# Ordinary identity matmuls in TensorE's planned gaps, ahead of the first scan and behind the last

## The chip, the cores and the metric

The kernel runs on one core of a Trainium2 chip. The core has a matrix engine (TensorE: PE, with its weight loads shown apart as PEld), VectorE (DVE), ScalarE (ACT), GpSimd (POOL) and SyncE (SP), which issues DMAs; POOL issues some DMAs too. The metric is the device time of one launch in microseconds, the median of several runs. A profile is one further execution with the hardware profiler on; its span goes from the first to the last instruction.

## The reference

The input is 8 batches of 1024 tokens with 256 features, in float32. Three blocks follow one another, each added to its input:

```
x = x + 0.5 * ffn(layernorm(x))
x = x + mamba(layernorm(x))
x = x + 0.5 * ffn(layernorm(x))

ffn:   gate = q(x) @ q(w_gate).T ;  up = q(x) @ q(w_up).T        # 256 -> 704
       out  = q(silu(gate) * up) @ q(w_down).T                   # 704 -> 256
       # q: blocks of 16 along the last axis, each rounded to an FP4 grid times (max |x| / 6)
mamba: x, z = split(norm(h) @ in_proj)                           # 256 -> 512 + 512
       x = silu(causal_conv4(x)) ; dt, B, C = split(x @ x_proj)  # 64 + 16 + 16
       delta = softplus(dt @ dt_proj + b)
       h_t = exp(delta_t * A) * h_(t-1) + delta_t * B_t * x_t    # per channel (512) and state (16)
       y_t = sum_n C_t[n] * h_t[n] + D * x_t ;  out = (y * silu(z)) @ out_proj
```

The recurrence over 1024 tokens runs on its own for every batch, channel and state.

## The kernel before

The tokens are cut into 16 chunks of 512, two to a batch. A chunk passes through five stages, written as generators: `stage_f1` (first feed-forward block, tiles `f_*`), `stage_m1` (norm, input projection, convolution, `x_proj`, `dt_proj`; tiles `m_*`), `stage_z` (the gate branch), `scan` (tiles `s_*`) and `stage_out` (output projection, tiles `o_*`, and the second feed-forward block, whose tiles are named `f_*` again). Ahead of all that, `prep_up` and `prep_down` quantize and transpose the weights (`w_ld`, `w_t`), and `prep_mamba` loads and scales the others.

In the scan, for each of 16 states and each of 4 groups of 128 channels, ACT forms `s_bu` (L793) and the decay `s_da` (L797), TensorE transposes `s_bu` into PSUM (`s_pb`, L800, against the identity `ident`), and DVE runs the recurrence over 512 tokens in one instruction (`s_h`, L802). POOL multiplies by C (L810) and adds the result to DRAM with an accumulating DMA (`accd`, L835).

In a feed-forward block, ACT normalizes (`f_xn`), `quant` rounds it with DVE, ACT and POOL in turn (L459 to L469), TensorE transposes (`f_pt`, L547), multiplies by both weights (`f_pg`, `f_pu`, L559, in two halves of 352 columns, two matmuls each), transposes the quantized product (`f_pa`, `f_pb`, L571 and L575) and multiplies by the down weights (`f_po`, L579, six matmuls of 256 columns). In the profile an ordinary float32 matmul is two records, a transpose is one.

All instructions are recorded first, and then `set_order` fixes the order of each engine. `Graph` collects the dependencies and prices every instruction (`price`), and `plan` is a list scheduler over the engines: it walks forward with priorities, then back and forward again, `PASSES` times, and the plan with the shortest total by its own prices is kept. Each engine's instructions are then chained in that order by dependencies without a semaphore. So each engine takes its instructions strictly in the planned order and waits wherever an operand isn't there yet.

The planner knows of TensorE's clock: it counts the columns that pass in each `TICK` (3413 ns), a transpose as half an ordinary matmul, and where the tick before had fewer than `WARM` columns, it doubles the price of the TensorE instruction:

```
if not back and e == ET.PE:
    if passed[t // TICK - 1] < WARM:
        more = hold
    passed[(t + hold + more) // TICK] += cols
    free[e] += more
```

Two PSUM buffers, pool `psb`, hold the transposes `s_pb` of the scan. `ident` is made by POOL as the first thing in the program.

## Time and profile before

| | us |
|---|---|
| runs shown (3) | 2523.82, 2534.21, 2535.66 |
| median | 2534.21 |
| the profiled execution | 2536.37 |
| its span | 2534.4 |
| PE busy | 2344.9 (93%) |
| DVE busy | 2184.4 (86%) |
| ACT busy | 2146.9 (85%) |
| POOL busy | 2177.2 (86%) |
| first transpose on TensorE (w_t, L490) starts | 19.05 |
| first scan instruction (L802) starts | 158.92 |
| last scan instructions (L802, two merged) | 2445.72, for 2.45 |

The mean granted TensorE clock is 0.985 of full speed. In a timeline, rows that follow each other with the same line and tiles are merged (xN, the time from the first start to the last end), and the brackets show the idle time ahead of the row and what ended it. In views of stretches, the columns are the stretch, its length, the busy time of each engine asked for (with its instructions), the granted clock (PEclk), the share of the DMA engines and the GB/s that they moved. The chain of waits follows the work back from the last instruction to what released each step.

### The profile page before, as it was taken

To read this page: it belongs to the slowest core of one execution; us is meant where nothing else is said; L and a number is where in the kernel's file an instruction comes from. 1 tells how busy PE (TensorE), PEld (TensorE's weight loads), DVE (VectorE), ACT (ScalarE), POOL (GpSimd) and SP (SyncE) were. 2 spreads that over 40 slices of the span, in tenths; PEclk is the share of its full clock that TensorE was granted. 3 is DMA by queue.
4 is the path that set the end of the run, shared out by engine and by line. 5 is a ranking of instruction groups with operands and counts; after the bars stand their busy time and mean duration, and the time that the engine had idled before them with its cause. 6 is when DMAs were issued, how large, how long until landed. Compare 5 with 4: busy or idle time off the path is not lost.

```text
span 2534.4 us, 33625 instructions
## 1 busy us (share of the span) xinstructions
PE 2344.9 (93%) x10980; PEld 1591.6 (63%) x10980; DVE 2184.4 (86%) x3082; ACT 2146.9 (85%) x3952; POOL 2177.2 (86%) x1556
## 2 busy tenths in 40 slices
PE   5989898999999999999999999999999999888876
PEld 3555565766666666666666666666666666655544
DVE  7568797998989899898989899898989989878885
ACT  4489787998989988999888989898989988999842
POOL 4359798899989999899998999899997999899952
PEclk9989999999999999999999999999999999999998
DMA  3049779699888988789897998889896988999950
GB/s 90 9 117 207 194 163 223 163 186 238 166 197 195 218 202 189 205 171 239 176 219 173 201 221 176 211 173 221 195 202 181 189 225 175 216 235 211 232 127 17
DMA packets 113647, 465.57 MB, mean 184 GB/s; under 512 B 14592, under 2 KB 32896, under 8 KB 76864
## 3 DMA queue, kind: packets, MB, share of 16 engines
q0 software_dynamic: 36576, 266.35, 56.3%
q1 hardware_dynamic: 76896, 197.08, 24.2%
q8 instruction: 86, 1.41, 0.2%
q14 instruction: 89, 0.73, 0.1%
HBM read 146.19 MB, written 317.19 MB: 183 GB/s over the span
## 4 chain that ended last, share of the span: by engine, by line
POOL 36%; PE 27%; issue 11%; DVE 9%; ACT 9%; DMA 8%; POOLq 0%; SPq 0%; DVEq 0%; ACTq 0%
POOL s_h L810 20%; PE f_pg L559 4%; PE f_pu L559 4%; PE f_po L579 4%; PE s_pb L800 4%; POOL accd L835 4%; DVE s_h L802 4%; DMA accd<-s_h 3%; PE m_pc L682 3%; POOL f_h L462 3%; POOL f_h L469 3%; ACT s_bu L793 2%; ACT s_da L797 2%; POOL f_xn L469 2%; POOL o_y L771 2%
## 5 line engine op out<-in xcount | busy, mean ns | idle before, releaser
L810 POOL TENSOR_TENSOR s_h<-s_h,s_cbc 128x1024 f32<-128x1024 f32 x512 | 1281.8, 2596 | 51.7 <-ACT s_carry L828 27.0
L797 ACT ACTIVATE s_da<-m_delta,an 128x512 f32<-128x512 f32 x1024 | 714.5, 715 | 44.5 <-DVE s_h L802 42.8
L793 ACT ACTIVATE s_bu<-m_duT,m_bc 128x512 f32<-128x512 f32 x1024 | 693.4, 715 | 15.6 <-PE s_pb L800 14.1
L800 PEld LDWEIGHTS s_pb<-ident,s_bu 128*128 128x128 f32 x4096 | 498.0, 142 | 330.2 <-issue 123.4
L800 PE MATMUL s_pb<-ident,s_bu 128*128 128x128 f32 x4096 | 639.2, 277 | 50.9 <-DVE s_h L802 47.4
L802 DVE TENSOR_TENSOR_SCAN s_h<-s_da,s_carry,s_pb 128x512 f32<-128x512 f32 x512 | 636.5, 1265 | 16.5 <-PE s_pb L800 13.3
L802 DVE TENSOR_TENSOR_SCAN s_h<-s_da,s_pb 128x512 f32<-128x512 f32 x512 | 604.4, 1206 | 35.0 <-PE s_pb L800 21.1
L579 PE MATMUL f_po<-wdn,f_ht 128*128 128x256 f32 x1536 | 393.1, 387 | 11.5 <-ACT f_ht L576 6.8
L559 PE MATMUL f_pg<-wg,f_xt 128*128 128x352 f32 x1024 | 370.5, 473 | 13.7 <-ACT f_xt L549 6.2
L559 PE MATMUL f_pu<-wu,f_xt 128*128 128x352 f32 x1024 | 365.6, 468 | 14.1 <-DVE f_h L563 8.4
L579 PEld LDWEIGHTS f_po<-wdn,f_ht 128*128 128x128 f32 x1536 | 276.1, 192 | 73.3 <-ACT f_ht L576 17.0
L835 POOL DMA_DIRECT2D accd<-s_h x238 | 230.7, 969 | 31.8 <-POOL s_h L810 24.1
L559 PEld LDWEIGHTS f_pu<-wu,f_xt 128*128 128x128 f32 x1024 | 182.6, 193 | 115.7 <-issue 34.5
L682 PE MATMUL m_pc<-m_xp,cdg 128*128 128x512 f32 x512 | 252.7, 595 | 2.4 <-ACT m_car L679 2.4
L469 POOL TENSOR_TENSOR f_h<-f_h,q_sc 128x704 f32<-128x704 f32 x128 | 206.5, 1616 | 54.9 <-DVE f_h L468 50.5
L559 PEld LDWEIGHTS f_pg<-wg,f_xt 128*128 128x128 f32 x1024 | 180.3, 195 | 93.4 <-issue 15.1
L462 POOL TENSOR_TENSOR f_h<-f_h,q_rc 128x704 f32<-128x704 f32 x120 | 184.9, 1541 | 22.7 <-DVE q_rc L461 21.9
L563 DVE SCALAR_TENSOR_TENSOR f_h<-f_h,f_pg 128x352 f32<-128x352 f32 x256 | 128.7, 506 | 86.4 <-ACT f_h L562 85.5
L460 POOL TENSOR_SCALAR q_sc<-q_mx 128x44 f32<-128x44 f32 (+2 forms) x198 | 98.0, 497 | 88.5 <-DVE q_mx L459 83.8
L564 DVE TENSOR_TENSOR f_h<-f_h,f_pu 128x352 f32<-128x352 f32 x256 | 129.5, 507 | 41.6 <-PE f_pu L559 39.9
L562 ACT ACTIVATE f_h<-f_pg 128x352 f32<-128x352 f32 x256 | 115.6, 456 | 48.1 <-PE f_pg L559 46.6
L776 PE MATMUL o_po<-outw,o_y 128*128 128x256 f32 x512 | 129.3, 387 | 5.5 <-POOL o_y L771 2.9
(110 smaller groups left out, 3299.6 us busy)
## 6 DMA issues: line engine op xcount, KB each, us to landing
accd<-s_h POOLq DMA_DIRECT2D x238, 1024.0 KB, 9.7
s_cbc<-cd SPq DMA_DIRECT2D x128, 512.0 KB, 5.6
accd<-m_ud SPq DMA_DIRECT2D x64, 256.0 KB, 9.3
accd<-s_h SPq DMA_DIRECT2D x16, 1024.0 KB, 6.8
szd<-m_tz SPq DMA_DIRECT2D x64, 256.0 KB, 6.8
o_y<-accd SPq DMA_DIRECT2D x16, 1024.0 KB, 9.9
o_y<-accd POOLq DMA_DIRECT2D x16, 1024.0 KB, 9.1
o_sz<-szd SPq DMA_DIRECT2D x30, 512.0 KB, 5.1
```

Of the source, the lines that this page charges most:

```text
L462: mul0.tensor_tensor(vb, vb, rc.unsqueeze(2).to_broadcast([P, g, BLK]), ALU.mult)
L469: mul1.tensor_tensor(vb, vb, sc.unsqueeze(2).to_broadcast([P, g, BLK]), ALU.mult)
L559: nc.tensor.matmul(dst, xt[:, c, :], w[:, c, hf * FH : (hf + 1) * FH], start=(c == 0), stop=(c == 1))
L564: nc.vector.tensor_tensor(hh, hh, pu, ALU.mult)
L579: nc.tensor.matmul(po, ht[:, k, :], wdn[:, k, :], start=(k == 0), stop=(k == NF - 1))
L682: nc.tensor.matmul(pc, cdg[:, dc, k, :], xp[:, k : k + n], start=(k == 0), stop=(k == KC - 1))
L793: nc.scalar.activation(b, duT[s][t], AF.Copy, scale=bcol[s][:, t, k : k + 1])
L797: nc.scalar.activation(da, delta[s][dc], AF.Exp, scale=an[:, dc, k : k + 1])
L800: nc.tensor.transpose(pb[:, t * P : (t + 1) * P], bu[t][:, dc * P : (dc + 1) * P], ident)
L802: nc.vector.tensor_tensor_scan(h[:, dc, :], da, pb, init, ALU.mult, ALU.add)
L810: eng_c.tensor_tensor(hv, hv, cbc.unsqueeze(1).to_broadcast([P, cm, n]), ALU.mult)
L835: nc.gpsimd.dma_start(accd[s][j, :, :, :n], h, accum_op=ALU.add)
```

## The change

132 matmuls of `ident` by `ident` (128 columns, float32, not in transpose mode) are added on TensorE, 80 at the start of the program and 52 at its end. All 80 write one PSUM tile from `psb`, all 52 another, and nothing reads them. They are left out of the graph that the planner orders. When its order is found, `set_order` looks at the planned gaps of TensorE: for each gap of over 350 ns that lies ahead of the first planned scan instruction, or over 2000 ns behind the start of the last, it puts `FILL` (half) of the gap's time, at 213 ns each, in front of the instruction that ends the gap. The first gap is taken to begin 2.2 ticks before the first TensorE instruction. What is left of the 80 goes ahead of everything, and what is left of the 52 behind everything.

The planner's doubled price for a thin tick now holds only once the first scan is planned and until the last one is. Elsewhere a TensorE instruction is priced at full clock.

```diff
--- before.py
+++ after.py
@@ -88,6 +88,8 @@
 PORT = 200
 SLACK = 20000
 WARM = 3060
+KEEP = (80, 52)
+FILL = 0.5
 BANK = 1 << 30
 LAG = {
     (ET.DVE, ET.DVE): 127, (ET.DVE, ET.PE): 130, (ET.DVE, ET.Activation): 120, (ET.DVE, ET.Pool): 150,
@@ -179,6 +181,7 @@
         self.eng = [i.engine for i in insts]
         self.engines = sorted(set(self.eng), key=str)
         self.dma = [type(i).__name__ == "InstDMACopy" for i in insts]
+        self.scan = [bool(getattr(i, "is_tensor_tensor_scan", False)) for i in insts]
         self.cost = []
         pred = [{} for _ in insts]
         users, seen = defaultdict(list), defaultdict(list)
@@ -271,6 +274,7 @@
         dma_free = 0.0
         held, holder = 0.0, None
         passed = defaultdict(float)
+        scans = [0, sum(self.scan)]
         for x in range(self.n):
             if not left[x]:
                 heapq.heappush(wait[eng[x]], (0.0, x))
@@ -312,11 +316,13 @@
                 held, holder = t + hold, e
             start[x] = t
             order.append(x)
+            if self.scan[x]:
+                scans = [scans[0] + 1, scans[1] - 1]
             if not queued:
                 free[e] = t + hold
             more = 0.0
             if not back and e == ET.PE:
-                if passed[t // TICK - 1] < WARM:
+                if scans[0] and scans[1] and passed[t // TICK - 1] < WARM:
                     more = hold
                 passed[(t + hold + more) // TICK] += cols
                 free[e] += more
@@ -337,19 +343,40 @@
 
 def set_order(tc, tags, nbuf):
     insts = [i for i in tc.nc.cur_bb.bb.instructions if type(i).__name__ != "BassTilePoolBoundary"]
+    idle = [i for i in insts if i.engine == ET.PE and "keep" in extent([a for a in i.outs if hasattr(a, "bass_ap")][0])[0]]
+    names = {i.name for i in idle}
+    insts = [i for i in insts if i.name not in names]
     g = Graph(insts, tags, nbuf)
     path = g.paths()
     found = [g.plan([x - WEIGHT * path[x] for x in range(g.n)])]
     for _ in range(PASSES):
         total, _, start = g.plan([-s - c[0] for s, c in zip(found[-1][2], g.cost)], back=True)
         found.append(g.plan([total - s - c[0] for s, c in zip(start, g.cost)]))
-    prev = {}
-    for x in min(found, key=lambda f: f[0])[1]:
-        e = g.eng[x]
-        if e in prev:
-            tc.add_manual_dep(insts[x], insts[prev[e]].name, mybir.DependencyInfo(
+    _, order, start = min(found, key=lambda f: f[0])
+    seqs = defaultdict(list)
+    for x in order:
+        seqs[g.eng[x]].append(x)
+
+    scans = [start[x] for x in order if g.scan[x]]
+    seq, pe = [], seqs.pop(ET.PE)
+    left = list(KEEP)
+    at = start[pe[0]] - 2.2 * TICK
+    for x in pe:
+        gap = start[x] - at
+        k = 0 if start[x] < scans[0] else 1 if at > scans[-1] + 2000 else None
+        if k is not None and gap > 350:
+            n = min(left[k], int(FILL * gap / 213))
+            left[k] -= n
+            seq += [None] * n
+        seq.append(insts[x])
+        at = start[x] + g.cost[x][0]
+    spare = iter(idle)
+    chain = [i or next(spare) for i in [None] * left[0] + seq + [None] * left[1]]
+    chains = [chain] + [[insts[x] for x in u] for u in seqs.values()]
+    for u in chains:
+        for i, j in zip(u, u[1:]):
+            tc.add_manual_dep(j, i.name, mybir.DependencyInfo(
                 mybir.DependencyClass.NoSync, mybir.DependencyReason.DATA), reason="issue order")
-        prev[e] = x
 
 
 @with_exitstack
@@ -404,6 +431,13 @@
     make_identity(nc, ident)
     mhalf = const.tile([P, NT], F32, name="mhalf")
     nc.gpsimd.memset(mhalf, -0.5)
+
+    def keep_warm(n):
+        w = psb.tile([P, T], F32, tag="psb", name="keep")
+        for _ in range(n):
+            nc.tensor.matmul(w[:, :P], ident, ident, start=True, stop=True)
+
+    keep_warm(KEEP[0])
 
     def cload(shape, src, name):
         t = const.tile(shape, F32, name=name)
@@ -861,6 +895,7 @@
         spread(stage_out(s), t0 + T_O, t0 + T_O + d, pf + 3, K_O if s >= S - KE else 1)
     for _, _, gen, kind[0] in sorted(work, key=lambda w: w[:2]):
         next(gen, None)
+    keep_warm(KEEP[1])
     set_order(tc, tags, nbuf)
```

In the built program, the keeps stand on TensorE as follows, in the stretch to the second `f_pt` and at the end (xN: so many instructions; the tiles' operands are left out):

```
keep x29, w_t x4, keep, w_t x2, keep x8, w_t x4, keep, w_t x2, keep x3, w_t x4, keep, w_t x2, keep x5,
w_t x4, keep, w_t x2, keep x3, f_pt x4, keep x2, f_pg x2, f_pu x4, f_pg x2, w_t, keep, w_t, f_pg x2,
w_t x4, keep, w_t x4, keep, w_t x2, f_pu x3, f_pg x2, f_pu, keep x9, f_pt x4, keep x2, f_pg x2, ...
...
f_pu x2, f_pg x2, f_pu x2, keep x2, f_pa x4, keep x2, f_pb x2, keep, f_po x6, o_po x2, keep, f_pa x4,
keep x2, f_pb x2, o_po, f_po x6, o_po x2, f_pa x4, o_po, keep, f_pb x2, keep, f_po x6, o_po x10,
keep x20, f_pt x4, keep x2, f_pg x2, f_pu x3, f_pg x2, f_pu, f_pg x2, f_pu x2, f_pg x2, keep x9, f_pu x2,
keep x3, f_pt x4, keep x2, f_pg x2, ... f_po x6, keep, f_po x6, keep, f_pa x4, f_pb x2, keep, f_po x6, keep x3
```

## The prediction

> **What bounds the kernel now.** I read first the page's summary of the 40 slices and its chain of waits.

> ```profile
> PE 2344.9 (93%) x10980; PEld 1591.6 (63%) x10980; DVE 2184.4 (86%) x3082; ACT 2146.9 (85%) x3952; POOL 2177.2 (86%) x1556
> ...
> PE   5989898999999999999999999999999999888876
> ...
> PEclk9989999999999999999999999999999999999998
> ...
> POOL 36%; PE 27%; issue 11%; DVE 9%; ACT 9%; DMA 8%; POOLq 0%; SPq 0%; DVEq 0%; ACTq 0%
> ```

> No engine is full: four of them stand at 85 to 93%, and the chain changes engine all the time. From 160 to 2447 us (scans running) the time is therefore set by how well the orders of all engines fit each other. The granted TensorE clock is near full there. Only ahead of the first scan (158.92 us) and behind the last (2448.2 us) are other engines slack and TensorE starved, so there I looked at stretches of the clock.

> ```profile
> 47.50:51.50 4.00, 0.80 (x6) 0.91 0.00 0
> 51.50:58.00 6.50, 6.50 (x12) 0.53 0.01 3
> ...
> 74.90:77.50 2.60, 0.97 (x7) 1.00 0.00 0
> 77.50:82.00 4.50, 4.48 (x13) 0.62 0.00 0
> ```

> The columns are the stretch, its length, TensorE's busy time, the granted clock, and DMA. After 4.0 us with six transposes the clock is at 0.53; after 2.6 us with a few of them it is at 0.62. What that costs is in TensorE's timeline:

> ```profile
> 46.27 1.35 PE L559 MATMUL f_pu<-wu,f_xt 128*128 128x352 f32 x4
> 50.13 0.66 PE L547 MATMUL f_pt<-ident,f_xn 128*128 128x128 f32 x4 [2.52 <-POOL f_xn L469]
> 51.47 2.71 PE L559 MATMUL f_pg<-wg,f_xt 128*128 128x352 f32 x4 [0.69 <-ACT f_xt L549]
> 53.98 2.55 PE L559 MATMUL f_pu<-wu,f_xt 128*128 128x352 f32 x4
> 56.33 1.98 PE L559 MATMUL f_pg<-wg,f_xt 128*128 128x352 f32 x4
> ...
> 2483.20 1.12 PE L547 MATMUL f_pt<-ident,f_xn 128*128 128x128 f32 x4 [7.80 <-POOL f_xn L469]
> 2485.01 2.71 PE L559 MATMUL f_pg<-wg,f_xt 128*128 128x352 f32 x4 [0.69 <-ACT f_xt L549]
> ...
> 2498.09 2.71 PE L559 MATMUL f_pu<-wu,f_xt 128*128 128x352 f32 x4 [3.09 <-DVE f_h L564]
> ```

> The same four records take 1.35 to 1.45 us warm and 2.71 cold. The clock view reads 1.00 in the first 40 us although f_pg at 33.31 also takes 2.71, so in that stretch I go by durations.

> Dense transposes do not bring the clock back: from 166.8 to 177.0 us TensorE is 92% busy with them (9.40 of 10.20 us) at a granted 0.50. The keep matmuls are ordinary ones, so they should count.

> **The gains, part by part.** In the chain of waits, the cold pieces ahead of the first scan are:
> - a, 31.5 to 38: f_pt 1.13 against 0.67, f_pg 2.71 against 1.45, f_pu 1.79 against 1.18: 2.33 us.
> - b, 51.5 to 58: 2.71 against 1.45, 2.35 and 1.77 against 1.18 each: 3.02 us.
> - c, f_po at 77.52: 4.54 against 2.86: 1.68 us.
> - d, f_po at 146.19: 4.54 against 2.86: 1.68 us.

> Behind the last scan: f_pu and o_po at 2450 (1.7 us), f_pt and f_pg at 2483 with the start of f_pu (1.87 us), and f_pu at 2498 (1.26 us). All together 13.5 us, half a percent: the most that the clock can give here.

> **Which of them the keeps reach.** A keep waits for nothing but ident, so it runs at the front of its gap, not spread over it. From the rows, spacing goes with columns: f_pg 352 columns 0.59 us, f_po 256 columns 0.43, m_pc 512 columns 0.86. A keep of 128 columns is then 0.215 us warm and 0.43 cold. No row shows an ordinary 128-column matmul, and each comes with two weight loads (median 0.190 us each), so the other bound is 0.38 warm. I take 0.215, as f_po's records run every 0.215 us with their loads beside them, and keep 0.38 for the range. In the built order:
> - 29 keeps stand ahead of everything. ident is ready at 1.3 us, so they are done by 13.8 us even when cold, and w_t starts at 19.05. They should do nothing.
> - 25 keeps lie among and behind the 24 w_t transposes. Before, that stretch (19.05 to 31.5) has 6.8 us of work and 5.7 idle. They fit warm (5.4 us) but not cold (10.75); the clock should come up half way. Gain a 2.33 us, cost 0.3.
> - 9 keeps ahead of the second f_pt and 2 behind it fill 2.4 of 4.0 us. Gain b in full, 3.02.
> - 3 keeps after f_po and one after f_pb cut c's stretch without ordinary matmuls from 2.6 to about 1.6 us. Gain 1.68. They fit the waits of 1.18 and 0.47 us.
> - 4 keeps stand behind f_pt and f_pa, ahead of m_dt: 2.1 us are left uncovered before them, so I count half of d, 0.84, and a delay of m_dt of 0.45 (0.86 us of keeps in a wait of some 0.4).
> - Single keeps: three among the L506 transposes (waits of 0.39 and 0.20), 0.2; one ahead of m_pd where there was no wait, 0.2; the others fit their waits.
> - Tail: none stands ahead of f_pu at 2450, gain 0. Two ahead of f_pa, where TensorE had no wait, cost 0.43; two ahead of f_pb, twice, in waits of 0.31 us, cost 0.24.
> - 20 keeps after o_po end near 2479.7 and leave 3.5 us idle up to f_pt, more than the 2.6 that was enough at c. Gain 0, bounds 0 and 1.87.
> - 9 keeps ahead of f_pu at 2498 leave 1.2 of 3.09 us. Gain 1.26.
> - Three behind the last f_po end 0.65 us after 2529.7, and the span ends at 2534.4: nothing.

> Gains 2.33 + 3.02 + 1.68 + 0.84 + 1.26 = 9.13; costs 0.3 + 0.45 + 0.2 + 0.2 + 0.43 + 0.24 = 1.82. Net 7.3 us saved. With 0.38 us a keep, the costs go to about 9 us (4.0 among w_t, 0.9 ahead of the second f_pt, 1.2 at m_dt, 0.9 at f_pb, the rest in small pieces) and the gains to 11.8, as 20 keeps would then fill the 7.8 us: net 2.6.

> The front saving should pass through: from 82 to 143 us TensorE is busy 60.36 of 61.40 us, it carries the chain, and the first scan waits for its transposes.

> The keeps' two PSUM tiles come from the two-buffer psb pool. The s_pb on the same buffer stands behind all keeps in TensorE's own queue, and the tail's keeps come after the last scan's read: no wait is added. No DMA, and no instruction of another engine, is added.

> [...] At c, 2.6 us without ordinary matmuls halved the clock. [...]

> **What moves.** The planner is a list scheduler, and its prices at both ends changed: TensorE instructions after a thin window cost double before, and now only between the scans. So it gives other orders everywhere. Between the built programs, 64% of TensorE's instructions in the first tenth stand at the same position, and 38 to 59% in the others. The work is the same, the fit is not. What an order is worth shows in this trace itself, as each batch is the same work in another order. The first scan of each batch:

> ```profile
> 158.92 1.22 DVE L802 TENSOR_TENSOR_SCAN s_h<-s_da,s_pb 128x512 f32<-128x512 f32 x1 [0.17 <-PE s_pb L800]
> 450.62 1.21 DVE L802 TENSOR_TENSOR_SCAN s_h<-s_da,s_pb 128x512 f32<-128x512 f32 x1
> 742.82 1.21 DVE L802 TENSOR_TENSOR_SCAN s_h<-s_da,s_pb 128x512 f32<-128x512 f32 x1
> 1034.80 1.21 DVE L802 TENSOR_TENSOR_SCAN s_h<-s_da,s_pb 128x512 f32<-128x512 f32 x1
> 1328.09 1.21 DVE L802 TENSOR_TENSOR_SCAN s_h<-s_da,s_pb 128x512 f32<-128x512 f32 x1
> 1618.67 1.21 DVE L802 TENSOR_TENSOR_SCAN s_h<-s_da,s_pb 128x512 f32<-128x512 f32 x1
> 1915.11 1.21 DVE L802 TENSOR_TENSOR_SCAN s_h<-s_da,s_pb 128x512 f32<-128x512 f32 x1
> ```

> The six intervals are 291.7, 292.2, 292.0, 293.3, 290.6 and 296.4 us: mean 292.7, spread 2.0. Two plans of seven such batches differ by about 2.0 x sqrt(14) = 7.5 us either way. I take zero, and bounds from the extremes: seven batches like the best, 7 x 2.1 = 15 us less; seven like the worst, 7 x 3.7 = 26 us more.

> **Sum.** The profiled execution took 2536.37 us, 2.2 above the median of the runs, 2534.21. It would go to 2529.1; against the median, 2526.9. I say 2527.

> **Rivals.**
> - The new orders fit worse (the other side). The scans' stage would show intervals near 296.4: 2534.2 - 7.3 + 26 = 2553. It makes the kernel measurably slower from 2.9 us a batch on ((12.7 + 7.3) / 7). For it: the 296.4 in the trace. Against: four of the six lie within 1.0 of the mean. Chance 0.18.
> - They fit better: 2534.2 - 7.3 - 15 = 2512. Beyond -0.5% from 0.8 us a batch on, which is well inside the spread of 2.0. Chance 0.32.
> - The keeps do not hold the clock, as they run at the front of gaps: only b is gained and the costs of 1.8 stay, 2533. For it: the rest of 3.5 us at 2479.7. Against: b and f_pu at 2498 leave only short rests. Chance 0.12.
> - A keep costs 0.38 us: net 2.6, 2531.6. Chance 0.10.
> - The forecast with a small effect of the orders: 0.28.

> **Range and chances.** 0.5% is 12.7 us, about what a measurement of this kernel can tell from no change (its three runs lie between 2523.82 and 2535.66). Faster takes the second rival, 0.32; same the last three, 0.50; slower 0.18. Spread of the orders 7.5, of the runs and of the clock's terms about 5 each: 10 in all, so 13 either way for 8 in 10 of the inner cases, 2514 to 2540. Reaching into the two outer rivals until 2 in 10 are left: 2511 to 2548.

> **What would show it.** Right: f_pg behind the first two f_pt at 1.45 and not 2.71; f_po at c at 2.86; f_pu ahead of the last f_pt at 1.45; f_pg behind the 20 keeps still near 2.7; w_t still starting cold; the first scan near 152.2 us (the front's share of the net, 7.87 - 1.15 = 6.7 us) instead of 158.9; a tail, last scan to end, about 0.6 us shorter than 86.2. Wrong: a first scan no earlier, batch intervals off 292.7 by over 2 us on average, keeps of 0.38 us.

## The result and the profile after

The changed kernel is slower, by 0.4%: 2544.88 us median against 2534.81 before (nine runs each), ratio 1.0041 with a 95% interval of 1.0023 to 1.0058. The forecast was 2527 us, a little faster than before, with a range of 2511 to 2548.

The head of the page after (busy times, granted clock, chain by engine):

```profile
PE 2381.3 (94%) x11244; PEld 1630.8 (64%) x11244; DVE 2187.1 (86%) x3082; ACT 2150.6 (84%) x3952; POOL 2175.4 (85%) x1556
...
PEclk9989999999999999999999999999999999999899
...
POOL 32%; PE 28%; issue 11%; DVE 10%; ACT 9%; DMA 9%; SPq 0%; POOLq 0%; DVEq 0%; ACTq 0%
```

TensorE's busy time grew by 36 us, 264 records for 132 keeps among them; the other engines' work is the same to a few microseconds. Yet the span is 11.4 us longer. TensorE's timeline after shows that most of what was forecast for both ends came about:

```profile
18.65 1.11 PE L524 MATMUL w_t<-ident,w_ld 128*128 128x128 f32 x4 [8.34 <-POOL w_ld L503]
...
46.44 2.17 PE L438 MATMUL keep<-ident 128*128 128x128 f32 x18
50.08 0.66 PE L581 MATMUL f_pt<-ident,f_xn 128*128 128x128 f32 x4 [1.47 <-POOL f_xn L503]
50.57 0.61 PE L438 MATMUL keep<-ident 128*128 128x128 f32 x4
51.42 1.45 PE L593 MATMUL f_pg<-wg,f_xt 128*128 128x352 f32 x4 [0.24 <-ACT f_xt L583]
...
74.53 2.86 PE L613 MATMUL f_po<-wdn,f_ht 128*128 128x256 f32 x12 [0.24 <-ACT f_ht L606]
...
2487.92 4.63 PE L438 MATMUL keep<-ident 128*128 128x128 f32 x40
2495.89 0.66 PE L581 MATMUL f_pt<-ident,f_xn 128*128 128x128 f32 x4 [3.34 <-POOL f_xn L503]
2496.38 0.61 PE L438 MATMUL keep<-ident 128*128 128x128 f32 x4
2497.23 2.23 PE L593 MATMUL f_pg<-wg,f_xt 128*128 128x352 f32 x4 [0.24 <-ACT f_xt L583]
...
2511.06 1.45 PE L593 MATMUL f_pu<-wu,f_xt 128*128 128x352 f32 x4 [1.57 <-DVE f_h L598]
```

f_pg behind the second f_pt takes 1.45 instead of 2.71, f_po at c 2.86 instead of 4.54, f_pu in the tail 1.45 instead of 2.71. f_pg behind the 20 keeps is still cold in part (2.23), and w_t still starts cold (1.11). The time went between the ends. The first scan of each batch, on DVE:

```profile
152.75 4.54 DVE L836 TENSOR_TENSOR_SCAN s_h<-s_da,s_pb 128x512 f32<-128x512 f32 x4
439.70 1.19 DVE L836 TENSOR_TENSOR_SCAN s_h<-s_da,s_pb 128x512 f32<-128x512 f32 x1
735.64 1.22 DVE L836 TENSOR_TENSOR_SCAN s_h<-s_da,s_pb 128x512 f32<-128x512 f32 x1
1027.39 1.21 DVE L836 TENSOR_TENSOR_SCAN s_h<-s_da,s_pb 128x512 f32<-128x512 f32 x1
1326.76 1.21 DVE L836 TENSOR_TENSOR_SCAN s_h<-s_da,s_pb 128x512 f32<-128x512 f32 x1
1619.59 1.22 DVE L836 TENSOR_TENSOR_SCAN s_h<-s_da,s_pb 128x512 f32<-128x512 f32 x1 [0.55 <-PE s_pb L834]
1929.39 1.21 DVE L836 TENSOR_TENSOR_SCAN s_h<-s_da,s_pb 128x512 f32<-128x512 f32 x1
```

The first scan is 6.2 us earlier than in the profile before, close to the 152.2 forecast. (An eighth batch follows in both kernels, at 2213.28 here and at 2197.32 before; see the part on the prediction.) The intervals are now 287.0, 295.9, 291.8, 299.4, 292.8 and 309.8 us, where they were 291.7, 292.2, 292.0, 293.3, 290.6 and 296.4. From the first scan to the end of the last one it took 2308.5 us against 2289.2 (the scans' stage from here on); from there to the end, the tail, 84.5 against 86.2. So -6.2 + 19.3 - 1.7 = 11.4 us, the whole difference of the spans.

What the longest interval (310 us) holds is seen in the chain of waits of the changed kernel, at its end:

```profile
1888.86 14.01 DMA x1d<-x4a
1902.88 12.23 DMA x4c<-x1d
1915.11 0.02 issue
1915.14 0.43 DVE bn_st L557
```

A chunk's feed-forward result goes to DRAM and comes back (26 us). DVE reaches the statistics of that chunk (`bn_st`) before it is back, and stands still for 7.1 us. Over the whole scans' stage, the waits of DVE for that load, in the kernel before and then after (us in total, times, longest):

```profile
DVE bn_st L523 <- DMA x4c<-x1d: 4.5, 4, 2.9
```

```profile
DVE bn_st L557 <- DMA x4c<-x1d: 23.1, 7, 7.1
```

That is one place where the new order fits worse. A wait of DVE isn't yet time of the kernel, so this view names a candidate. Whether it was the orders, and whether by rule or by luck, was for experiments.

### The profile page after: what moved, and what is told of

It is laid out like the page before. It is cut to its first block, busy times and chain, and to the rows that moved or that the text cites. A ratio compares the mean times of both kernels' runs of the same rounds, so it can differ in the third digit from the quotient of the medians.

```text
span 2545.8 us, 34158 instructions
## 1 busy us (share of the span) xinstructions
PE 2381.3 (94%) x11244; PEld 1630.8 (64%) x11244; DVE 2187.1 (86%) x3082; ACT 2150.6 (84%) x3952; POOL 2175.4 (85%) x1556
## 3 DMA queue, kind: packets, MB, share of 16 engines
HBM read 146.19 MB, written 317.19 MB: 182 GB/s over the span
## 4 chain that ended last, share of the span: by engine, by line
POOL 32%; PE 28%; issue 11%; DVE 10%; ACT 9%; DMA 9%; SPq 0%; POOLq 0%; DVEq 0%; ACTq 0%
POOL s_h L844 17%; PE f_po L613 5%; DVE s_h L836 5%; PE f_pg L593 5%; PE f_pu L593 4%; PE s_pb L834 4%; POOL accd L869 3%; DMA accd<-s_h 3%; POOL f_h L503 3%; POOL f_h L496 3%; ACT s_da L831 2%; ACT s_bu L827 2%; PE m_pc L716 2%; PE o_po L810 2%; DMA x4c<-x1d 2%
## 5 line engine op out<-in xcount | busy, mean ns | idle before, releaser
L831 ACT ACTIVATE s_da<-m_delta,an 128x512 f32<-128x512 f32 x1024 | 718.0, 719 | 42.7 <-DVE s_h L836 41.5
L494 POOL TENSOR_SCALAR q_sc<-q_mx 128x44 f32<-128x44 f32 (+2 forms) x198 | 99.1, 506 | 87.1 <-DVE q_mx L493 82.1
L596 ACT ACTIVATE f_h<-f_pg 128x352 f32<-128x352 f32 x256 | 116.0, 458 | 56.4 <-PE f_pg L593 54.8
L774 PE MATMUL m_pz<-m_hnT,inw 128*128 128x512 f32 x256 | 128.6, 601 | 3.7 <-ACT m_delta L743 3.3
```

The lines of the kernel that those rows point to most:

```text
L831: nc.scalar.activation(da, delta[s][dc], AF.Exp, scale=an[:, dc, k : k + 1])
```

## The experiments

**Theory A**: keeps work at the ends as forecast; the new orders cost the time between the scans. **Theory B**: the keeps themselves slow what comes later. The price rule and the keeps were taken apart.

### Keeps on the old order

```diff
-                if scans[0] and scans[1] and passed[t // TICK - 1] < WARM:
+                if passed[t // TICK - 1] < WARM:
```

> All keeps, but the planner doubles its price in a thin tick everywhere, as in the kernel before; every engine's order of the other instructions is then the one of before, and keeps also land in gaps that only the doubled price makes (14 more single ones between f_pg and f_pu). Theory A (the keeps work as forecast at both ends, and what was lost is the fit of the new orders between the scans): first scan near 154, from the first scan to the end of the last one 2289 us as before (2308 in the changed kernel), tail near 85, ratio to before 0.9965 to 0.998. Theory B (the keeps themselves slow what comes after, by the clock or by PSUM or instruction traffic): the scans' stage near 2308, ratio near 1.004.

Ratio 1.0011 (0.9997 to 1.0026); in its profile the first scan is at 153.34, the stage 2292.7, the tail 85.3. Apart from the keeps, PE, DVE, ACT and POOL take their instructions here in the order of before. The stage is near that of before, not 2308: against B. The total gained nothing, where A expected 0.9965 to 0.998.

In the next one a gap is measured from the doubled end (`at = start[x] + cost + extra[x]`, where `extra` holds what the thin tick added), so that no keep separates f_pg from f_pu (in part):

```diff
-        at = start[x] + g.cost[x][0]
+        at = start[x] + g.cost[x][0] + extra[x]
```

> As the run with the old prices, but a gap is counted from the doubled end of a thin tick's instruction, so that no keep stands between f_pg and f_pu. Order of the rest as in the kernel before. Theory A: first scan near 152.5, scans' stage 2289, tail near 85, ratio 0.9965 (-8 to -9 us). Theory B: ratio near 1.004.

Ratio 0.9994 (0.9981 to 1.0007), first scan 152.31, stage 2290.5, tail 87.1. The changed kernel's loss is gone, but of the 8 us expected under A at most 5 are there.

Then the longest gap of the tail was filled further (in part):

```diff
-            n = min(left[k], int(FILL * gap / 213))
+            n = min(left[k], int((0.9 if k and gap > 6000 else FILL) * gap / 213))
-KEEP = (80, 52)
+KEEP = (80, 72)
```

> As the run with true gaps, but gaps behind the last scan of over 6 us in the plan are filled to 0.9 instead of 0.5: 36 keeps instead of 20 stand ahead of the tail's first f_pt, 36 x 0.22 = 7.9 us against a wait of 7.8. If the clock falls there because the keeps end 3.3 us too early, f_pg behind it goes from 2.2 us to 1.45 and the tail gets 0.8 us shorter, or 0.3 if the keeps hold f_pt up by some tenths. If the keeps don't hold the clock by themselves: f_pg stays at 2.2. Ratio 0.996.

Ratio 0.9994 (0.998 to 1.0009), as without the longer row of keeps, where 0.996 was expected; tail 84.8. The timelines of the run with true gaps, and then of this one, at the long gap:

```profile
2471.26 4.63 PE L440 MATMUL keep<-ident 128*128 128x128 f32 x40
2479.23 1.11 PE L583 MATMUL f_pt<-ident,f_xn 128*128 128x128 f32 x4 [3.34 <-POOL f_xn L505]
2480.13 1.06 PE L440 MATMUL keep<-ident 128*128 128x128 f32 x4
2481.03 2.71 PE L595 MATMUL f_pg<-wg,f_xt 128*128 128x352 f32 x4
```

```profile
2475.16 8.20 PE L440 MATMUL keep<-ident 128*128 128x128 f32 x72
2483.20 0.60 PE L583 MATMUL f_pt<-ident,f_xn 128*128 128x128 f32 x4
2483.64 0.61 PE L440 MATMUL keep<-ident 128*128 128x128 f32 x4
2484.49 1.45 PE L595 MATMUL f_pg<-wg,f_xt 128*128 128x352 f32 x4 [0.24 <-ACT f_xt L585]
```

Twenty keeps end 3.3 us too early and the clock falls; 36 reach to f_pt and hold it. It recurs: f_pg took 1.54 to 2.71 us in the six profiles with 20 keeps there, 1.45 in both with 36, and 2.71 in all ten with none. The tail is 2.3 us shorter in this pair of profiles, but the tails with 20 keeps on this order differ by 2 us among themselves (85.1 to 87.1), and the total shows no gain.

### The price rule without keeps

```diff
-KEEP = (80, 52)
-    keep_warm(KEEP[0])
-    keep_warm(KEEP[1])
+KEEP = (0, 0)
```

> The planner's change alone: no keep, order of all other instructions as in the changed kernel. Theory A: the ends lose what the keeps gave (7.8 us) and the scans' stage stays at 2308: 2552 us, ratio 1.007. Theory B: scans' stage back to 2289, ratio near 1.000.

Ratio 1.0086 (1.0064 to 1.0109), stage 2306.1, and the batch of 310.9 us is there without a keep. That decides for theory A as to the loss: the new orders alone cost 0.86%, 22 us, and the keeps on those orders win back 0.45% (1.0086 to 1.0041, uncertain by 0.3).

### The kernel before once more, and the ends apart

> The kernel before, unchanged, profiled once more, to see how much its parts vary from one execution to the next. If the keeps' 6 us at the front are lost again between the scans, this profile has a scans' stage near 2285 (the first profile, 2289, was then a slow one: it is 2 to 4 us above the median of the runs). If they are not lost, the stage is 2289 to 2292 as in the three kernels with keeps and the old orders. First scan 158.9 and tail 86 in both cases.

2529.88 us, span 2527.9. The first scan of this execution:

```profile
155.61 4.55 DVE L802 TENSOR_TENSOR_SCAN s_h<-s_da,s_pb 128x512 f32<-128x512 f32 x4 [0.18 <-PE s_pb L800]
```

That is 3.3 us earlier than in the profile that the forecast was made from. The granted clock says why (the stretches of 3.41 us on whose bounds it changes in this execution; length, TensorE's busy time, clock):

```profile
47.69:51.10 3.41, 0.66 (x4) 1.00 0.00 0
51.10:54.51 3.41, 3.23 (x6) 0.50 0.03 5
54.51:57.92 3.41, 3.41 (x14) 1.00 0.00 0
74.99:78.40 3.41, 2.94 (x17) 1.00 0.00 0
78.40:81.81 3.41, 3.16 (x17) 1.00 0.38 154
```

At b the clock was low for one piece of 3.41 us and not for two, and at c it did not fall: f_po takes 2.86 us there, where it took 4.54. The stage is 2286.1.

Keeps at one end alone, in the true gaps (`KEEP = (80, 0)` and `(0, 52)`, the other call of `keep_warm` left out):

> Keeps ahead of the first scan only, true gaps, old prices, order of the rest as before. First scan 152.3 as with both. If the front's gain passes through the scans' stage: ratio 0.9975 (-6.6). If the scans' stage takes it back (its start is not what it waits for): ratio 0.999 to 1.000, with a stage longer by as much as the start is earlier.

Ratio 1.0023 (1.0007 to 1.0039), first scan 152.33, stage 2295.5.

> Keeps behind the last scan only. First scan 158.9, stage as before, tail 85 to 87 as with both: ratio 0.9995 to 1.0003, whichever theory holds for the front.

Ratio 0.9997 (0.9977 to 1.0017), first scan 155.4, stage 2279.9, tail 85.1. The front's keeps bring no gain in the total; in this run it is 0.23% longer.

### Other orders of the same work

A planner constant changed by a little gives another order: with WAIT at 31, over half of TensorE's instructions stand elsewhere.

```diff
-WAIT = 30
+WAIT = 31
```

> The changed kernel with one planner constant, WAIT, at 31 instead of 30: keeps and the new price rule as they are, the orders reshuffled (half of TensorE's instructions at another position). If the loss between the scans is the luck of one order, the stage falls anywhere in 2285 to 2310, and the long batch of 310 us (from 1620 to 1929) is gone: ratio 0.996 to 1.004. If the new price rule makes worse orders as such, the stage is again near 2308, ratio 1.004 or above.

Ratio 1.0016 (0.9996 to 1.0037), stage 2301.4, tail 76.8, longest batch 297.1 us.

The same without keeps, and with the old rule (`LOOK = 610` in place of 600 in two of them):

> The kernel before (no keeps, old price rule) with WAIT at 31 instead of 30: another order of the same work, by the same rule. It and the next three give four further orders, two by each rule. If orders differ by luck: ratios of both rules lie anywhere between 0.995 and 1.009, overlapping. If the new rule makes worse orders as such: the two by the old rule lie within 0.997 to 1.003 and the two by the new rule above 1.004.

> As the run before, with LOOK at 610 instead of 600. Luck: anywhere in 0.995 to 1.009. Rule: 0.997 to 1.003.

> The new price rule without keeps, WAIT at 31: the order of the earlier run with keeps at WAIT 31 (ratio 1.0016). If the keeps are worth the 0.45% that they were worth on the changed kernel's order, the ratio is 1.006; if they are worth nothing, as on the old order, 1.0016. Luck of orders: this order, between 1.001 and 1.006, is nearer to the kernel before than the changed one's (1.0086). Rule: above 1.004.

> The new price rule without keeps, LOOK at 610. Four fifths of TensorE's instructions stand where the changed kernel has them. Luck: anywhere in 0.995 to 1.009, most likely near the changed kernel's 1.0086, as the orders are alike. Rule: above 1.004.

All orders without keeps, with the stage and the tail of their profiles in us:

| order | ratio to before | 95% interval | stage | tail |
|---|---|---|---|---|
| old rule (the order of before; three executions without front keeps, one of them with the tail's) | 1 | | 2279.9 to 2289.2 | 85 to 86 |
| old rule, WAIT 31 | 1.0054 | 1.0038 to 1.0071 | 2302.8 | 82.4 |
| old rule, LOOK 610 | 1.0064 | 1.0047 to 1.0080 | 2307.9 | 80.8 |
| new rule | 1.0086 | 1.0064 to 1.0109 | 2306.1 | 86.6 |
| new rule, WAIT 31 | 1.0034 | 1.0022 to 1.0047 | 2304.4 | 78.4 |
| new rule, LOOK 610 | 1.0099 | 1.0085 to 1.0114 | 2305.5 | 85.2 |

Neither forecast held as it was put: the old rule's two lie above 1.003, one of the new rule's below 1.004, and the 1.0099 lies above the range given for luck. The rules overlap, so the new rule isn't shown to make worse orders as such. But the order of before is the best of six, and clearly: the other five stand at 1.0067 on average, 17 us, with a spread of 0.0026. Their scans' stages are all 2303 to 2308. The five aren't quite independent (four fifths of TensorE's instructions in the last one stand where the changed kernel has them), and nothing here says how the order of before came to be so good.

What in the orders costs the time is open; two candidates each explain a part at most. The first is the clock. Clock time lost (the span times one minus the mean granted clock, mean over a kernel's runs) is 42.7 us with the order of before and 59.5 with the new rule; with LOOK at 610 it is 54.8 (old rule) and 60.8 (new). So these three lose 12 to 18 us more to the clock, and their spans are 16 to 23 us longer. But the two orders with WAIT 31 lose 43.7 and 38.1, about as much as before or less, and are 13 and 9 us longer all the same. Nor do these sums say which is the cause, since the clock fell behind pieces in which TensorE streamed 0.40 of the time or less (last section), and a TensorE that waits more may well have more of these. The second candidate is waiting for DMAs: in the stage, DVE and POOL wait for them 17 to 29 us in the ten profiles with the order of before, and 33 to 53 in the eight with others. The wait of DVE for x4c, 23.1 us in the changed kernel, is 25.0 us with the new rule alone, 19.8 and 12.1 with WAIT 31 and 15.0 and 6.5 with LOOK 610 (old and new rule), against 2.4 to 7.0 with the order of before. The 6.5 belongs to the slowest order of all, so that one wait isn't what makes an order slow.

### Does the front pass through?

Thirty keeps right in front of the first s_pb (`first` below), and none elsewhere; the old price rule (in part):

```diff
+        if x == first:
+            seq += [None] * KEEP[0]
```

> The order of before, and 30 keeps (30 x 0.22 = 6.6 us) right in front of the first transpose of the scan, where TensorE had no wait: a pure delay of the first scan by some 6 us, no clock to be won. If time at the front passes through: ratio 1.0022 to 1.0028. If the scans' stage absorbs it: ratio 1.000 to 1.001, stage some 5 us shorter than in the kernel before.

Ratio 1.0015 (1.0002 to 1.0027), +3.8 us, between the two theories; first scan 162.22, stage 2284.4. Set against the mean of the three executions in the table, 2285.1, the stage isn't shorter, which would speak for passing through; the ratio doesn't decide.

> The keeps ahead of the first scan alone, once more (first time 1.0023). The profiles of the old order without front keeps have first scans at 158.9, 155.6 and 155.4, those with at 152.3 to 153.5, so they are worth some 4 us. If that passes through: ratio 0.998 to 0.999, and the 1.0023 was scatter. If not: 1.000 to 1.002.

Ratio 1.0012 (0.9995 to 1.0030), first scan 152.33, stage 2285.4.

> Keeps at both ends with the long gap filled, once more (first time 0.9994). Front 4 us and tail 1.5 us, if they pass through: 0.9975 to 0.9985. If only the tail's does: 0.999 to 1.000.

Ratio 0.9994 (0.9978 to 1.0011) again: only the tail's, if any.

> The old price rule at WAIT 31 with keeps in the true gaps; without keeps it was 1.0054. Keeps worth 0.45% as on the changed kernel's order: 1.001. Worth 0.15 to 0.2% as on the new rule's order at WAIT 31: 1.0035. Worth nothing: 1.0054.

Ratio 1.0054 (1.0036 to 1.0072), as without keeps.

So the keeps of both ends are worth 0.45, 0.18, 0.06 and 0.00% on the four orders where they were measured, about 0.17% or 4 us on average, each with an uncertainty of some 0.15 to 0.3. (The 0.06 is that of the true gaps; with the single keeps between f_pg and f_pu it was a loss of 0.11.) On the order of before, the front's keeps alone never showed a gain (1.0023 and 1.0012), although the first scan comes 3 us earlier. Six profiles with front keeps have stages of 2285.4 to 2295.5, mean 2291.8; three without have a mean of 2285.1. So the lead seems to be given back between the scans. How much is not settled, since the stages of each group scatter by 3 to 5 us, and neither is why: the delay run, which should tell, lies between both answers, and the grid on which the clock changes lay differently in the executions (last section).

No version here is measurably faster than the kernel before; keeps on its own order (0.9994) are as fast, and half a percent faster than the changed kernel.

## Why the prediction was wrong, step by step

- **"I take zero, and bounds from the extremes"** for the new orders is the step that failed. The order of the changed kernel alone, without a keep, costs 0.86%, 22 us. The five reshuffled orders have a mean of +0.67%, 17 us, and scatter by 0.26%, 6.6 us. So the size of the scatter was about right (7.5 us between two plans, where 6.6 us each makes some 9), but its centre was not zero. The batches from which I took the spread all belong to the same plan. They show how much batches of one plan differ, not how good that plan is among plans. With that centre and the keeps' 4 us the sum would be 2535 + 17 - 4 = 2548; measured were 2544.88.
- **That the 7.5 us came out near** was in part luck. The list of first scans left out the eighth batch; with its interval of 282.2 us the spread of the intervals is 4.4 instead of 2.0, and 16 us stand in place of the 7.5. This interval is short in all 18 profiles (278.5 to 287.7), so it tells more of the batch's place than of the order.

```profile
2197.32 2.33 DVE L802 TENSOR_TENSOR_SCAN s_h<-s_da,s_pb 128x512 f32<-128x512 f32 x2
```

- **The rival with the new orders**, priced from 296.4 us a batch, had the right mechanism: the six intervals after average 296.1. Its 2553 was 8 us too high, and its chance of 0.18 too low, as all five reshuffles cost time. That 2544.88 lies within 2511 to 2548 is owed to the reach into this rival.
- **The gains at the front (2.33 + 3.02 + 1.68 + half of 1.68 us)** were right against that one profile: first scan 152.75, forecast 152.2. But that execution had an unlucky clock: in the other executions of this order without front keeps a, b and d recur, c does not, and b is shorter. Against 155.4 to 155.6 the front is worth 3 us. An average over executions was needed and I had one.
- **"The front saving should pass through"**: not shown. On the old order front keeps gain nothing in the total (1.0023 and 1.0012); what takes it back is not settled.
- **20 keeps leave 3.5 us idle, gain 0**: nearly. f_pg stayed cold in part, but f_pt and f_pg together took 0.9 us less than before (0.66 and 2.23 against 1.12 and 2.71), and 36 keeps held the clock. The row of c, from which the 0 was taken, was a fair guide: after 3.34 us idle the clock fell.
- **"Dense transposes do not bring the clock back"**: wrong. The very stretch that was shown for it ends with the clock coming back, at 177.05 us, behind transposes alone (last section). Whether keeps in transpose mode would have done as well, no run tried. And of the "six transposes" at b, four are transposes; one f_pu and one f_pg record lie on the edges.
- **29 keeps at the start do nothing**: right. They end at 10.3 us and w_t starts cold.
- **0.215 us a keep**: close. In the rows of 20 and 36 a keep starts every 0.223 us, and cold every 0.427. The bound of 0.38 is out.
- **d, half counted**: it was kept warm, f_po takes 2.76 us there.
- **Tail, 0.6 us shorter**: 1.7 in the changed kernel, 0.9 of it at f_pt and f_pg. Tails of one order differ by such amounts from execution to execution: 86.2 to 88.1 in the order of before without tail keeps, 85.1 to 87.1 with 20 keeps at the long gap.

## What to carry to other kernels

When an order comes out of a heuristic planner, any edit to its prices can deal the whole order again. The expected price of that is the distance from the present order to the mean of the orders, not zero; here it was 17 us. Keep the plan fixed and insert such helpers afterwards, or measure several neighbours of the plan before judging the edit. And a clock that falls by chance is priced from several executions.

## What the runs showed of the hardware

```profile
74.66:78.07 3.41, 1.76 (x11) 1.00 0.00 0
78.07:81.48 3.41, 3.41 (x10) 0.50 0.00 0
```

```profile
71.58:74.99 3.41, 2.23 (x13) 1.00 0.00 0
74.99:78.40 3.41, 2.94 (x17) 1.00 0.00 0
```

In the first the grid puts both waits into one piece, and the clock falls behind it; in the second it divides them between two pieces.

For all 18 profiles I summed, for each piece of the grid, the time that its records stream: a record counts 0.833 ns a column at full clock and twice that in the low state, where f_pg (352 columns) comes every 0.587 us and f_po (256) every 0.427; at full clock they come every 0.296 and 0.216 (medians of the first profile of the kernel before). The start of each profile is left out, up to the first change that it records, as the clock reads 1.00 there whatever the durations (f_pg at 33.31 us in the first profile of the kernel before takes 2.71). Behind 249 pieces the full clock fell, and none of them had streamed over 0.40 of the piece; behind 12506 it stayed, and none of these had under 0.35. In the first profile of the kernel before and the changed kernel's together these are 31 pieces, none over 0.40, and 1385, none under 0.36. In the low state it rose again from about 0.75 of what that state can stream; between 0.72 and 0.78 it rose behind some pieces and stayed low behind others (in the same two profiles the lowest piece with a rise behind it had 0.72, the highest without one 0.77).

Transposes, counted by their columns, fit these sums in both directions. 104 pieces with nothing but transposes stayed warm, and of the 249 rises, 7 came behind a piece with nothing but transposes (in those two profiles 16, and 2 of 31). One is in the profile that the forecast was made from, at the end of the stretch shown for the opposite:

```profile
173.64:177.05 3.41, 3.21 (x14) 0.50 0.79 163
177.05:180.47 3.42, 2.38 (x13) 1.00 0.36 151
```

The two pieces ahead of that, from 166.82 to 173.64 us, hold nothing but transposes too (four of them, 0.85 us cold, come every 1.25 us). They streamed 0.69 and 0.73 of what the low state can, and the clock stayed low; the piece shown streamed 0.77, and it rose. So that they are transposes, as the prediction had it, isn't what kept the clock low.

The clock also goes along with much of the scatter between runs. In three sets of 29 runs of the kernel before, the span follows the clock time lost with correlations of 0.71, 0.72 and 0.84, and 0.8 to 1.1 us of span for each us lost; in a fourth set, of 11 runs, the correlation is 0.37. Which drives which isn't shown by that.
